# A fill on GpSimd after each gather, and one four-bank PSUM tile for the counts of a step, in a recommendation model's kernel

## The chip, the cores and the metric

The kernel runs on one core of a Trainium2 chip. The metric is the device time of that core in microseconds (us), the median of the runs shown.

## The reference

For each of 16384 rows the model averages 32 word vectors of 300 numbers, averages 20 vectors of 64 numbers from each of three tables, takes one vector of 64 from each of four small tables, and feeds the 748 numbers through three layers. Beside this it sums one scalar per lookup (the "wide" part).

```python
tok = word_emb[token_idx].mean(axis=1)          # 50000 x 300, 32 per row
e1 = emb_mh1[mh1_idx].mean(axis=1)              # 1000 x 64, 20 per row
e2 = emb_mh2[mh2_idx].mean(axis=1)              # 5000 x 64
e3 = emb_mh3[mh3_idx].mean(axis=1)              # 10000 x 64
o1, o2, o3, o4 = emb_oh1[oh1_idx], ...          # 100, 50, 20, 1000 x 64
emb = concatenate([tok, e1, e2, e3, o1, o2, o3, o4], axis=1)
wide = wide_mh1[mh1_idx].sum(...) + ... + wide_oh4[oh4_idx][:, 0]
h = relu(emb @ W1 + b1)                         # 748 x 1024
h = relu(h @ W2 + b2)                           # 1024 x 512
h = relu(h @ W3 + b3)                           # 512 x 256
return sigmoid(h @ Wd + bd + wide)
```

## The kernel before

The batch is cut into 128 tiles of 128 rows. The main loop (L444) runs over tiles, and each tile has 11 steps (`STEPS`), of which each handles six rows from each half of the tile (`ONEHOT` = 6; the last step has four). Three streams are woven together by hand: the framework keeps the order in which the instructions are written, and `Paced` (L411) spreads a stream's work evenly over the steps.

The word vectors come by gather. `tokens` (L205) issues, for each of the 32 words of a tile, one indirect DMA from GpSimd's queue (L212) that fetches 128 rows of 300 numbers. Two gathers share a buffer `tok_rows`, of which there are six. With a lag of three pairs, `add_up` (L197) adds the two halves and then adds them to `g`, both on VectorE (L202, L203). Sixteen pairs are spread over 11 steps.

The small tables stay on the chip, split into 138 slices of 128 rows (`n_h` = 138) and held as three bf16 terms. For each row of the batch, the kernel counts how often each table entry is looked up. `one_hots` (L272) builds, on VectorE, two one-hot arrays for six rows of both halves: `row1` (entry within a slice) and `slice1` (which slice), one step ahead, in two buffers. `counts` (L288) multiplies them: for each row one matmul of 64 x 128 by 64 x 138 into the PSUM tile `pc`, 12 in a full step (L298). A `pc` tile has two banks, one for each half of the tile, and takes three rows of each; so a step of six rows fills two `pc` tiles, and ScalarE evicts each with one ACTIVATE of 828 columns (L305) to `cnt`, fp8. There are two `pc` tiles in the pool `ps_c`. The last step's four rows go as three and one.

One tile later, `small_sums` (L313) multiplies the counts with the tables' terms: 138 matmuls of 195 columns per tile (L323) into `pg`, followed by a VectorE sum of the three terms (L330).

The layers run on blocks of four tiles. `transposed` (L358) turns the block's `g` with TensorE (L366) and scales it on VectorE (L367). `mlp` (L388) and `layer` (L368) then run 88 matmuls of 512 columns in fp32 per block (L376; two records each in the trace), with ReLU evictions on ScalarE (L385), spread over the steps of the next block, and a last layer at L399 to L403. The first block's layers start after the fourth tile's counts are summed; the last blocks are cut smaller (two tiles, one, one).

[...] In a step the written order is: one-hots of the next step, this step's count matmuls and evictions, gathers with older sums, small-table sums, layer matmuls.

Of the kernel before, what the change touches and what calls it, by code (L numbers as in the profile page):

```python
# [8 lines left out]
F32 = mybir.dt.float32  # L9
# [4 lines left out]
AF = mybir.ActivationFunctionType  # L14
# [3 lines left out]
P = 128  # L18
# [3 lines left out]
D1, D2, D3 = 1024, 512, 256  # L22
TOK_GROUP = 2
TOK_LAG = 3
BLOCK = 512
HALF = P // 2
N_SMALL = 3 * N_MH + 4
# [17 lines left out]
def kernel(  # L45
# [21 lines left out]
    nc = tc.nc  # L67
    B = out.shape[0]
    NSUB = BLOCK // P
    M1, M2, M3 = D1 // P, D2 // P, D3 // P  # L70
# [3 lines left out]
    slices, n_h = {}, 0  # L74
    for f in SMALL:
        n = -(-tables[f].shape[0] // P)
        slices[f] = (n_h, n_h + n)
        n_h += n
    PER_BANK = 512 // n_h

    tokp = ctx.enter_context(tc.tile_pool(name="tok", bufs=2 * TOK_LAG))
    const = ctx.enter_context(tc.tile_pool(name="const", bufs=1))
# [6 lines left out]
    wp = ctx.enter_context(tc.tile_pool(name="wide", bufs=2 * NSUB))  # L89
    xp = ctx.enter_context(tc.tile_pool(name="x", bufs=1))  # L90
    ps_h = ctx.enter_context(tc.tile_pool(name="ps_h", bufs=2, space=bass.MemoryType.PSUM))
    ps_c = ctx.enter_context(tc.tile_pool(name="ps_c", bufs=2, space=bass.MemoryType.PSUM))
    ps_g = ctx.enter_context(tc.tile_pool(name="ps_g", bufs=2, space=bass.MemoryType.PSUM))


# [16 lines left out]
    scale = const.tile([P, NK], F32, name="scale")  # L112
# [14 lines left out]
    at = 0  # L127
# [65 lines left out]
            nc.sync.dma_start(out=sb, in_=dram)  # L193

    under_way = []

    def add_up(rows, g, first):  # L197
        a, b, n = rows[:, 0:TOK_D], rows[:, TOK_D : 2 * TOK_D], TOK_D
        if first:
            nc.vector.tensor_add(g[:, 0:n], a, b)  # L200
        else:
            nc.vector.tensor_add(a, a, b)  # L202
            nc.vector.tensor_add(g[:, 0:n], g[:, 0:n], a)  # L203

    def tokens(g, it):  # L205


        for q in range(N_TOK // TOK_GROUP):
            rows = tokp.tile([P, TOK_GROUP * TOK_D], F32, name="tok_rows")
            for t in range(TOK_GROUP):  # L210
                j = q * TOK_GROUP + t
                nc.gpsimd.indirect_dma_start(  # L212
                    out=rows[:, t * TOK_D : (t + 1) * TOK_D],
                    out_offset=None,
                    in_=word,
                    in_offset=bass.IndirectOffsetOnAxis(ap=it[:, j : j + 1], axis=0),
                )
            under_way.append((rows, g, q))
            if len(under_way) > TOK_LAG:
                rows, to, old_q = under_way.pop(0)  # L220
                add_up(rows, to, old_q == 0)
            yield 1
# [5 lines left out]
    def load_indices(blk):  # L228


        b0 = blk * BLOCK
        it = idxp.tile([P, NSUB, N_TOK], I32, name="it")
        nc.sync.dma_start(
            out=it, in_=idx[b0 : b0 + BLOCK, 0:N_TOK].rearrange("(s p) c -> p s c", p=P)
        )
# [36 lines left out]
    def one_hots(sc, s, i):  # L272

        b = i * ONEHOT
        rows = min(ONEHOT, HALF - b)
        row1 = ohp.tile([P, ONEHOT, P], BF16, name="row1")
        slice1 = ohp.tile([P, ONEHOT, n_h], BF16, name="slice1")
        for w, (one, n) in enumerate(((row1, P), (slice1, n_h))):
            shape = [P, rows, n // 2, 2]
            nc.vector.tensor_tensor(  # L280
                one[:, 0:rows, :].rearrange("p i (n d) -> p i n d", d=2),
                iota[:, 0:n].rearrange("p (n d) -> p n d", d=2).unsqueeze(1).to_broadcast(shape),
                sc[:, s // 2, w, s % 2, b : b + rows, :].unsqueeze(2).to_broadcast(shape),
                ALU.is_equal,
            )
        return row1, slice1

    def counts(cnt, hot, i):  # L288

        b = i * ONEHOT  # L290
        rows = min(ONEHOT, HALF - b)
        for k0 in range(0, rows, PER_BANK):
            n = min(PER_BANK, rows - k0)
            pc = ps_c.tile([P, 2, 512], F32, name="pc")
            for k in range(n):
                for f in range(2):
                    half = slice(f * HALF, (f + 1) * HALF)
                    nc.tensor.matmul(  # L298
                        pc[:, f, k * n_h : (k + 1) * n_h],
                        hot[0][half, k0 + k, :],  # L300
                        hot[1][half, k0 + k, :],
                        start=True,
                        stop=True,
                    )
            nc.scalar.activation(  # L305
                cnt[:, :, b + k0 : b + k0 + n, :].rearrange("l f k h -> l f (k h)"),
                pc[:, :, 0 : n * n_h],
                AF.Copy,
                scale=0.5,
                saturate=True,  # L310
            )

    def small_sums(g, cnt):  # L313

# [43 lines left out]
    def transposed(gs):  # L358

        n = len(gs) * P  # L360
        x = xp.tile([P, NK, BLOCK], F32, name="x", tag="even")
        for k in range(NK):
            kk = chunk_k[k]
            pt = ps_h.tile([P, BLOCK], F32, name="pt", tag="ph")
            for s, g in enumerate(gs):
# [6 lines left out]
    def layer(dst, weights, bias, src, kks, n_out, n):  # L372
        for m in range(n_out):
            ph = ps_h.tile([P, BLOCK], F32, name="ph", tag="ph")
            for k, kk in enumerate(kks):
# [66 lines left out]
    hot = one_hots(sc, 0, 0)  # L442
    gs, wides, layers, before, b0 = [], [], None, None, 0
    for t in range(tiles + 1):  # L444
# [4 lines left out]
        if t < tiles:  # L449
            if s == 0 and t:  # L450
                it, sc = next_it, next_sc
            g = gp.tile([P, G_COLS], F32, name="g")
            cnt = cp.tile([P, 2, HALF, n_h], FP8, name="cnt", tag="counts")
            toks = Paced(tokens(g, it[:, s, :].bitcast(U32)), N_TOK // TOK_GROUP, STEPS)
        else:
            last_tokens()
        for i in range(STEPS):
            if t < tiles:
                hot_now = hot
                if s == 1 and i == 0 and t + NSUB < tiles:  # L460
                    next_it, ix = load_indices(t // NSUB + 1)
                if s == 2 and i == 0 and t + NSUB < tiles + 1:
                    next_sc = lookup_keys(ix)
                if i < STEPS - 1:
                    hot = one_hots(sc, s, i + 1)
                elif t + 1 < tiles:
                    hot = one_hots(next_sc if s == NSUB - 1 else sc, (s + 1) % NSUB, 0)
                counts(cnt, hot_now, i)
                if t == 0 and i % 3:
                    next(tables_on_chip, None)  # L470
                if t == 0 and i == STEPS - 1:
                    load_weights()
                toks.go()
            if sums:
                sums.go()
            if layers:
                layers.go()
# [55 lines left out]
```

## Time and profile before

| | |
|---|---|
| plain runs | 5515.67, 5517.34, 5519.1 us; median 5517.34 |
| profiled execution, its own time | 7368.99 us |
| span of the profile | 7367.2 us, mean granted TensorE clock 0.891 |
| busy, TensorE matmul / VectorE / ScalarE / GpSimd | 5894.3 / 3606.2 / 2632.3 / 4079.8 us |
| share of the span | 80% / 49% / 36% / 55% |
| DMA | 652.52 MB, of it 629.41 MB by the gathers' queue, 31.1% of 16 engines' span |

The profiled execution took 1852 us more than a plain one, so its totals and shares don't hold for plain runs as they stand. A row of the page's groups names line, engine and operation, what is written and read, the shape and the count, then busy time and mean of one (ns), then the idle time just before and what ended most of it. PE is TensorE, DVE VectorE, ACT ScalarE, POOL GpSimd; a trailing q is an engine's sequencer or queue. "issue" is time in which an engine waited for nothing that the profile shows.

### The profile page before, as it was taken

To read this page: it belongs to the slowest core of one execution; us is meant where nothing else is said; L and a number is where in the kernel's file an instruction comes from. 1 tells how busy PE (TensorE), PEld (TensorE's weight loads), DVE (VectorE), ACT (ScalarE), POOL (GpSimd) and SP (SyncE) were. 2 spreads that over 40 slices of the span, in tenths; PEclk is the share of its full clock that TensorE was granted. 3 is DMA by queue.
4 is the path that set the end of the run, shared out by engine and by line. 5 is a ranking of instruction groups with operands and counts; after the bars stand their busy time and mean duration, and the time that the engine had idled before them with its cause. 6 is when DMAs were issued, how large, how long until landed. Compare 5 with 4: busy or idle time off the path is not lost.

```text
span 7367.2 us, 103052 instructions
## 1 busy us (share of the span) xinstructions
PE 5894.3 (80%) x41320; PEld 3527.7 (48%) x41320; DVE 3606.2 (49%) x8013; ACT 2632.3 (36%) x3408; POOL 4079.8 (55%) x4103
## 2 busy tenths in 40 slices
PE   3688788878778888878888888888888788888789
PEld 2444444444444444444444444444444444444457
DVE  5544454445454454445444544454445454545443
ACT  4333333333333333333333333333333333333333
POOL 5555555555555555555555555555555555555552
PEclk8789888899898998889888889888988898888999
DMA  5333333333333333333333333333333333333331
GB/s 138 89 90 91 87 87 88 87 90 85 89 86 90 90 88 90 86 89 86 93 86 88 87 90 91 87 87 89 89 89 89 86 90 90 86 91 87 90 87 45
DMA packets 245345, 652.52 MB, mean 89 GB/s; under 512 B 108978, under 2 KB 111989, under 8 KB 244864
## 3 DMA queue, kind: packets, MB, share of 16 engines
q0 software_dynamic: 196608, 629.41, 31.1%
q1 hardware_dynamic: 48255, 16.53, 1.0%
q8 instruction: 323, 5.29, 0.3%
q14 instruction: 159, 1.29, 0.1%
HBM read 645.59 MB, written 0.07 MB: 88 GB/s over the span
## 4 chain that ended last, share of the span: by engine, by line
PE 52%; another core or an unknown queue 26%; ACT 13%; issue 5%; DVE 3%; POOL 0%; DMA 0%; DVEq 0%; SPq 0%; ACTq 0%; POOLq 0%
PE ph L376 24%; PE pg L323 17%; ACT cnt L305 12%; PE pc L298 9%; ACT h L385 1%; PE pt L366 1%; DVE x L367 1%; PE po L399 1%; DVE g L330 0%; PE po L403 0%; DVE slice L280 0%; DVE tok_rows L202 0%; DVE g L203 0%; ACT terms L166 0%
## 5 line engine op out<-in xcount | busy, mean ns | idle before, releaser
L212 POOL DMA_INDIRECT tok_rows<-in_word_emb_dram,it x4096 | 4078.9, 996 | 3207.7 <-DVE g L203 2195.9
L305 ACT ACTIVATE cnt<-pc 128x828 fp8e3<-128x828 f32 (+1 forms) x2816 | 2224.6, 842 | 3325.2 <-PE pc L298 1393.4
L323 PE MATMUL pg<-terms,cnt 128*128 128x195 bf16 x17664 | 2135.3, 271 | 272.0 <-issue 257.2
L280 DVE TENSOR_TENSOR row<-iota,sc 128x768 bf16<-128x768 bf16 (+1 forms) x1408 | 764.7, 543 | 2673.5 <-remote 1282.8
L323 PEld LDWEIGHTS <-cnt 128*128 128x128 fp8e3 x17664 | 1759.2, 147 | 502.7 <-issue 363.6
L298 PE MATMUL pc<-slice,row 64*128 64x138 bf16 x16384 | 880.2, 232 | 1047.6 <-ACT cnt L305 883.0
L376 PE MATMUL ph<-x,w_sb 128*128 128x512 f32 (+5 forms) x3264 | 1625.2, 626 | 43.7 <-issue 41.5
L298 PEld LDWEIGHTS <-row 64*128 64x128 bf16 x16384 | 570.1, 97 | 2182.3 <-issue 1611.2
L376 PE MATMUL ph<-h,w_sb 128*128 128x512 f32 (+2 forms) x2720 | 1404.9, 645 | 26.5 <-issue 24.7
L203 DVE TENSOR_TENSOR g<-g,tok_rows 128x300 f32<-128x300 f32 x1920 | 904.6, 471 | 65.6
L202 DVE TENSOR_TENSOR tok_rows<-tok_rows 128x300 f32<-128x300 f32 x1920 | 890.4, 464 | 0.0
L376 PEld LDWEIGHTS ph<-x,w_sb 128*128 128x128 f32 (+1 forms) x3264 | 610.5, 211 | 516.7 <-issue 505.3
L280 DVE TENSOR_TENSOR slice<-iota,sc 128x828 bf16<-128x828 bf16 (+1 forms) x1408 | 803.8, 571 | 0.0
L385 ACT ACTIVATE h<-ph,b_sb 128x512 f32<-128x512 f32 (+2 forms) x476 | 315.4, 663 | 1225.4 <-remote 739.8
L376 PEld LDWEIGHTS ph<-h,w_sb 128*128 128x128 f32 x2720 | 524.4, 217 | 422.9 <-issue 420.5
L330 DVE TENSOR_REDUCE g<-pg 128x130 f32<-128x390 f32 (+1 forms) x512 | 249.8, 509 | 827.9 <-remote 392.0
L367 DVE TENSOR_SCALAR x<-pt,scale 128x512 f32<-128x512 f32 (+4 forms) x204 | 140.9, 717 | 111.1 <-PE pt L366 104.4
L366 PE MATMUL pt<-ident,g 128*128 128x128 f32 (+1 forms) x768 | 124.8, 292 | 51.8 <-DVE x L367 51.4
L366 PEld LDWEIGHTS pt<-ident,g 128*128 128x128 f32 (+1 forms) x768 | 84.5, 143 | 91.7 <-DVE x L367 83.8
L305 ACT ACT_TABLE_LOAD x32 | 41.1, 1283 | 145.8 <-PE pc L298 145.0
L399 PE MATMUL po<-h,wd_sb 128*1 128x512 f32 (+2 forms) x136 | 62.0, 573 | 0.6 <-issue 0.3
L200 DVE TENSOR_TENSOR g<-tok_rows 128x300 f32<-128x300 f32 x128 | 59.2, 463 | 0.0
(32 smaller groups left out, 346.4 us busy)
## 6 DMA issues: line engine op xcount, KB each, us to landing
tok_rows<-in_word_emb_dram,it POOLq DMA_INDIRECT x4096
ix<-in_idx_dram SPq DMA_DIRECT2D x128, 32.0 KB
w_sb<-in_W_dram SPq DMA_DIRECT2D x6, 512.0 KB
it<-in_idx_dram SPq DMA_DIRECT2D x32, 64.0 KB
w_sb<-in_W_dram SPq DMA_DIRECT2D x1, 2048.0 KB
raw<-in_mh_dram SPq DMA_DIRECT2D x1, 975.0 KB
out_dram<-h SPq DMA_DIRECT2D x31, 2.0 KB
raw<-in_mh_dram SPq DMA_DIRECT2D x1, 292.5 KB
```

The lines of the kernel that those rows point to most:

```text
L202: nc.vector.tensor_add(a, a, b)
L203: nc.vector.tensor_add(g[:, 0:n], g[:, 0:n], a)
L212: nc.gpsimd.indirect_dma_start(out=rows[:, t * TOK_D : (t + 1) * TOK_D], out_offset=None, in_=word, in_offset=bass.IndirectOffsetOnAxis(ap ...
L280: nc.vector.tensor_tensor(one[:, 0:rows, :].rearrange("p i (n d) -> p i n d", d=2), iota[:, 0:n].rearrange("p (n d) -> p n d", d=2).unsque ...
L298: nc.tensor.matmul(pc[:, f, k * n_h : (k + 1) * n_h], hot[0][half, k0 + k, :], hot[1][half, k0 + k, :], start=True, stop=True,)
L305: nc.scalar.activation(cnt[:, :, b + k0 : b + k0 + n, :].rearrange("l f k h -> l f (k h)"), pc[:, :, 0 : n * n_h], AF.Copy, scale=0.5, sat ...
L323: nc.tensor.matmul(pg[:, j, :], by_slice[:, :, h], terms[:, h, :], start=(h == h0), stop=(h == h1 - 1))
L330: nc.vector.tensor_reduce(g[:, at : at + n * ROW].rearrange("p (f d) -> p f d", f=n), pg[:, 0:n, :].rearrange("p f (c d) -> p f d c", c=3) ...
L366: nc.tensor.transpose(pt[:kk, s * P : (s + 1) * P], chunk(g, k), ident)
L367: nc.vector.tensor_scalar(x[:kk, k, 0:n], pt[:kk, 0:n], scale[:kk, k : k + 1], None, ALU.mult)
L376: nc.tensor.matmul(ph[:, 0:n], weights[:kk, k, m * P : (m + 1) * P], src[:kk, k, 0:n], start=(k == 0), stop=(k == len(kks) - 1),)
L385: nc.scalar.activation(dst[:, m, 0:n], ph[:, 0:n], AF.Relu, bias=bias[:, m : m + 1])
```

## The change

Two edits are made together. After each gather, GpSimd fills an SBUF tile `pause` of 128 partitions by 128 fp32 columns with zeros; nothing reads the tile. And the counts of a step go into one `pc` tile of four banks: two for each half of the tile, each bank holding half of the step's rows (three, or two in the last step). One ACTIVATE of 1656 columns (1104 in the last step) evicts all of it. The pool `ps_c` now has one buffer in place of two, so it holds four banks as before.

```diff
+PAUSE = 128
-    PER_BANK = 512 // n_h
-    ps_c = ctx.enter_context(tc.tile_pool(name="ps_c", bufs=2, space=bass.MemoryType.PSUM))
+    ps_c = ctx.enter_context(tc.tile_pool(name="ps_c", bufs=1, space=bass.MemoryType.PSUM))
+    pause = const.tile([P, PAUSE], F32, name="pause")
 def tokens(g, it):
...
                 nc.gpsimd.indirect_dma_start(
...
                 )
+                nc.gpsimd.memset(pause, 0.0)
 def counts(cnt, hot, i):
...
-        for k0 in range(0, rows, PER_BANK):
-            n = min(PER_BANK, rows - k0)
-            pc = ps_c.tile([P, 2, 512], F32, name="pc")
-            for k in range(n):
-                for f in range(2):
-                    half = slice(f * HALF, (f + 1) * HALF)
-                    nc.tensor.matmul(
-                        pc[:, f, k * n_h : (k + 1) * n_h],
-                        hot[0][half, k0 + k, :],
-                        hot[1][half, k0 + k, :],
-                        start=True,
-                        stop=True,
-                    )
-            nc.scalar.activation(
-                cnt[:, :, b + k0 : b + k0 + n, :].rearrange("l f k h -> l f (k h)"),
-                pc[:, :, 0 : n * n_h],
-                AF.Copy,
-                scale=0.5,
-                saturate=True,
-            )
+        n = rows // 2
+        pc = ps_c.tile([P, 2, 2, 512], F32, name="pc")
+        for k in range(rows):
+            for f in range(2):
+                half = slice(f * HALF, (f + 1) * HALF)
+                at = k % n * n_h
+                nc.tensor.matmul(
+                    pc[:, f, k // n, at : at + n_h],
+                    hot[0][half, k, :],
+                    hot[1][half, k, :],
+                    start=True,
+                    stop=True,
+                )
+        nc.scalar.activation(
+            cnt[:, :, b : b + rows, :].rearrange("l f (g k) h -> l f g (k h)", g=2),
+            pc[:, :, :, 0 : n * n_h],
+            AF.Copy,
+            scale=0.5,
+            saturate=True,
+        )
```

## The prediction

> **What bounds the kernel now.** I read the page first, then the chain of waits, then a timeline of all engines in mid-kernel, then GpSimd alone, because the profiled execution took 7369 us (span 7367.2) and the three plain runs 5517. A rate may be taken from this profile only where the profile itself does not stretch it.
>
> ```profile
> PE 52%; another core or an unknown queue 26%; ACT 13%; issue 5%; DVE 3%; POOL 0%; DMA 0%; DVEq 0%; SPq 0%; ACTq 0%; POOLq 0%
> L212 POOL DMA_INDIRECT tok_rows<-in_word_emb_dram,it x4096 | 4078.9, 996 | 3207.7 <-DVE g L203 2195.9 <-issue 876.6 <-DVE g L200 64.8
> L305 ACT ACTIVATE cnt<-pc 128x828 fp8e3<-128x828 f32 (+1 forms) x2816 | 2224.6, 842 | 3325.2 <-PE pc L298 1393.4
> ```
>
> 26% of the span, 1915 us, hangs on a releaser that the profile does not know. One such piece, from the chain in order of time (start, length, what):
>
> ```profile
> 3742.11 1.61 ACT cnt L305 x2
> 3743.72 3.76 another core or an unknown queue
> 3747.49 0.02 issue
> ```
>
> 7367 less 1915 is 5452, within 1.2% of the plain median, so I take these stalls to be what profiling adds (inferred) and work with stretches that lie between them. Here is one (start, length, engine, line, out<-in, count, idle before):
>
> ```profile
> 3720.79 0.54 PE L298 MATMUL pc<-slice,row 64*128 64x138 bf16 x12
> 3721.19 1.61 ACT L305 ACTIVATE cnt<-pc 128x828 fp8e3<-128x828 f32 x2 [1.58 <-PE pc L298]
> 3721.26 1.34 PE L323 MATMUL pg<-terms,cnt 128*128 128x195 bf16 x13
> 3722.45 1.91 PE L376 MATMUL ph<-x,w_sb 128*128 128x512 f32 x4
> ...
> 3724.28 0.54 PE L298 MATMUL pc<-slice,row 64*128 64x138 bf16 x12
> 3724.65 0.95 POOL L212 DMA_INDIRECT tok_rows<-in_word_emb_dram,it  x1 [0.30 <-DVE g L203]
> ...
> 3725.90 0.95 POOL L212 DMA_INDIRECT tok_rows<-in_word_emb_dram,it  x1 [0.30 <-issue]
> ...
> 3727.16 0.95 POOL L212 DMA_INDIRECT tok_rows<-in_word_emb_dram,it  x1 [0.30 <-issue]
> ```
>
> Two rates are to be seen. TensorE repeats a step every 3.49 us (3720.79 to 3724.28) without a hole. GpSimd starts a gather every 1.25 us, also without a hole: the 0.30 us before each belongs to it, since it is there whatever the gather waited for. A step needs 32/11 = 2.91 gathers, so 3.64 us at 1.25. GpSimd is the slower of the two.
>
> Over the kernel: in the 3544 gathers that follow the one before by no more than 0.35 us, start-to-start averages 1.308 us (0.302 gap, 1.003 gather). 4096 x 1.308 = 5357. The last gather starts 80 us before the end and about 20 us are lost in the first tile (one 18.3 us wait for the first sum). 5357 + 80 + 20 = 5457, 60 below the plain 5517; 1.322 us per gather would close it. TensorE: 1408 steps x 3.49 = 4914, plus per block of four tiles some 8 us of transposes and last layer (3708.5 to 3716.3), x 32 = 250, plus about 120 idle in the first five tiles: 5290. So GpSimd is **full to about 1%**, and TensorE has some 200 us to spare. The busy share of the page (POOL 55%) hides this: it leaves out the gap and is diluted by the stalls. The same dilution makes GpSimd look idle behind VectorE:
>
> ```profile
> POOL tok_rows L212 <- DVE g L203: 2195.9, 1064, 9.8
> PE pc L298 <- ACT cnt L305: 883.0, 621, 8.1
> ```
>
> These rows (total us, times, longest) consist mostly of waits of 2 us and more, which is the length of the stalls; between them the waits are absent.
>
> **What the Trainium skill says.** GPSIMD Engine Reference, 3.1 (Elementwise), gives 1.03 cycles per element for a simple body, and 2.1 (Instruction dispatch) tens of cycles of software per instruction. Estimate for 128 columns at the 1.2 GHz that it states: 110 ns plus 25 to 70. The trace has a 128-column fill of 205 ns and one-column fills of 99 to 119, so 96 ns for 127 columns: it agrees. Perfetto Trace Analysis, section DMA Instruction — SWDGE (GPSIMD), says that DSPs 0 and 1 write the descriptors and that the gather's row ends when the last has done so; its section on GPSIMD instructions says to time by start-to-start spacing, which I do. ScalarE: Activation LUTs, What ACT_TABLE_LOAD costs, prices an ACTIVATE with immediates at 186 ns + 0.833 per element: 876 for 828, the trace has 863.
>
> **Part 1, 4096 fills.** One `memset` of 128x128 f32 after each gather, on the engine that has nothing to spare. It adds no DMA and no reader, and nobody waits for `pause`. A fill over an older fill may wait for that one, which ended a gather earlier: nothing. What queues behind it is the next gather, hence its landing, the VectorE sums, and the one-hots that stand behind the sums in VectorE's queue, hence TensorE. The rows that price it are at the kernel's start (GpSimd alone):
>
> ```profile
> 0.28 0.10 POOL L518 MEMSET const-float32-1.0<- 128x1 f32 x1
> 0.30 0.11 POOL L518 MEMSET const-bfloat16-1.0<- 128x1 bf16 x1
> 0.33 0.12 POOL L518 MEMSET const-uint8-127<- 128x1 uint8 x1
> 0.74 0.20 POOL masks.py:197 MEMSET ident<- 128x128 f32 x1 [0.29 <-POOLq L518]
> 0.99 0.23 POOL L121 IOTA iota_i<- 128x138 int32 x1
> ```
>
> One-column fills start 20 to 30 ns apart though each lasts 100, so the tail of a fill overlaps the next instruction. A 128-column one then occupies about 0.03 + 0.096 = 0.125 us; its whole row is 0.205; the IOTA after it starts 0.25 later. Below these lies zero, if the fill fits in the 0.30 us gap; above, 0.205 + 0.302 = 0.507, if the gap is paid twice; a gain is excluded only for this part, since it adds work to the full engine. I choose **0.165**, between occupancy and whole row. 4096 x 0.165 = 676 us, all on the path. The period becomes about 1.32 + 0.165 = 1.49, or 4.32 us per step, against TensorE's 3.49.
>
> A small credit: gathers take 0.945 us where VectorE rests and up to 1.15 beside its two-input sums. VectorE's work is unchanged and spread over a longer time, so the mean lengthening (about 0.06 us) shrinks by some 10%: 4096 x 0.006 = 25, of which I take 15.
>
> **Part 2, the counts of a step.** Removed: 2816 ACTIVATEs (2688 of 863 ns, 128 of 408). Added: 1280 of 1656 columns and 128 of 1104. At 186 + 0.833 per column these are 1.57 and 1.11 us. A full step goes from the 1.61 seen for the pair to 1.57: 0.04 less on ScalarE, which has slack (36% busy). TensorE's 12 matmuls stay. New is the wait: with one buffer of four banks in place of two of two, the first count matmul of a step waits for the previous step's eviction, and the layer and sum matmuls queue behind it. The eviction now starts after 12 matmuls instead of 6, some 0.6 us into the step in place of 0.40, and ends near 2.2; the next count matmul stands 3.49 after the first now, 4.3 after the change. Slack 1.3 us, and still about 1.0 when a 0.69 us `h` eviction just ahead delays it. Worth 0. In tiles 1 to 4, without layers, the gathers set 3.8 us and more per step, so the cover holds there. In tile 0, ScalarE also converts tables at 1.47 us each; a delay of up to 1 us in 11 steps is at most 11 us. If the fills were free and the cover thinner, 0.2 us per step would be 280 us, of which the 200 spare in TensorE takes most. I count 0, with -5 to +11.
>
> **Sum.** On the plain median: 5517 + 676 - 15 + 0 = 6178 us, 12% slower. In the profiled execution the same fills may partly vanish into waits that are there anyway: 7369 plus 0 to 676, perhaps 7700.
>
> **Rivals.**
> *The fill is free (not slower).* In the 0.30 us between gathers, if this gap is the sequencer preparing the next gather while the cores rest, a fill of 0.125 to 0.205 fits in. It decides as long as the fill is shorter than the gap. For it: the gap is constant. Against it: gathers released late by VectorE also start about 0.27 us after the release (3738.58 to 3738.86), where the fill at 0.74 starts together with the first work of ScalarE, so the gap looks like gather code on the cores; and GpSimd's sequencer already runs its 17 ns wait for a later gather at 14.0, just after a gather began at 13.88. Time: 5517, with -10 to +11. A partial fit (0.05 us left) gives 5720.
> *The gap is paid twice.* Alternating two kinds of instruction could cost a second start. For it: no row shows a gather after a fill. Against it: fill to IOTA is 0.25 in all. Time: 5517 + 4096 x 0.507 = 7594; half of the gap, 0.35, gives 6950.
> *TensorE is the bound, GpSimd isn't.* Then GpSimd's own sum at the lowest price rules: 4096 x (1.308 + 0.125) + 100 = 5970, still slower.
> *The single buffer stalls TensorE.* Priced above; behind gathers at 4.3 us per step it would need a wait over 0.6 us in every step to show.
>
> **How the numbers follow.** A measurement of this kernel tells about 0.2% (11 us) from no change. Serial fill at 0.105 to 0.25 us (5930 to 6540): 0.72. Free fill: 0.11, of which 0.08 within 0.2% and 0.03 faster. Partial fit: 0.05. Dearer than 0.25: 0.12. Slower in all: 0.89. The range 5890 to 6750 leaves out the free and most of the partly hidden case below, and part of the dear case above: about 0.2.
>
> **What would show it.** Right: start-to-start of gathers rises from 1.25 to 1.38-1.50 between stalls, with 4096 fills in between; TensorE shows waits before `pc` or one-hots that trace back to VectorE sums and gathers; one ACTIVATE of about 1.57 us per step, ending over 1 us before the next `pc`. Wrong: spacing still near 1.25 (free fill) or over 1.6 (gap twice); TensorE waiting for L305's eviction in ordinary steps between stalls (part 2 is not free).

## The result, and the profile after

The changed kernel takes 5879 us (median of four runs, 5876 to 5884) against 5517 for the kernel before: ratio 1.0657, 95% interval 1.0638 to 1.0675, slower by 362 us. Forecast were 6178 us, 661 more than before, and a range of 5890 to 6750: the direction and the engine were right, the amount was about 1.8 times too large.

The chips fall into two kinds: one runs the kernel before in 5516 to 5525 us, the other in some 7180 to 7250 (a single execution took 9409), and the profile of before shown above (7369 us) is like the second kind while the plain runs above and the profile after are like the first.

The page of the changed kernel: the chain by engine, then the groups (line, engine, operation, out<-in, count, busy us, mean ns, idle before).

```profile
POOL 44%; DMA 28%; DVE 11%; issue 8%; PE 8%; POOLq 0%; ACT 0%; DVEq 0%; SPq 0%; ACTq 0%
...
L214 POOL DMA_INDIRECT tok_rows<-in_word_emb_dram,it x4096 | 4129.0, 1008 | 773.9 <-issue 556.8
L308 ACT ACTIVATE cnt<-pc 128x1656 fp8e3<-128x1656 f32 (+1 forms) x1408 | 2122.4, 1507 | 2466.6 <-PE pc L301 2280.2
...
L220 POOL MEMSET pause<- 128x128 f32 x4096 | 905.9, 221 | 2.2
```

The chain runs through GpSimd, the landing of its gathers and VectorE's sums. The unknown releaser is gone from it. 4129.0 + 905.9 + 773.9 + 2.2 = 5811 of the span's 5882 us are accounted for by gathers, fills and the idle time before them. Of the 4095 stretches between the end of a gather and the start of the next, 4041 have the same length, 0.384 us; the other 54 add up to 118 us; most stand in the first 80 us and the last 125 us of the gathers, the rest are one of 1.0 to 1.7 us every 150 us or so. So GpSimd is full from the first gather to the last, but for some 100 us. GpSimd alone (start, length, ..., idle before):

```profile
3005.03 0.22 POOL L220 MEMSET pause<- 128x128 f32 x1
3005.42 1.01 POOL L214 DMA_INDIRECT tok_rows<-in_word_emb_dram,it  x1 [0.16 <-issue]
3006.42 0.22 POOL L220 MEMSET pause<- 128x128 f32 x1
3006.81 0.95 POOL L214 DMA_INDIRECT tok_rows<-in_word_emb_dram,it  x1 [0.17 <-issue]
3007.75 0.23 POOL L220 MEMSET pause<- 128x128 f32 x1
3008.14 0.95 POOL L214 DMA_INDIRECT tok_rows<-in_word_emb_dram,it  x1 [0.16 <-DVE g L204]
```

Two undisturbed gathers now start 1.33 us apart (6.81 to 8.14), where they started 1.25 apart before. The fill follows the gather at once; after it the next gather waits 0.17 us, where it used to wait 0.30 after a gather. So a fill whose row, its own length in the profile, is 0.22 us makes the period longer by only 0.08. All engines in the same stretch:

```profile
3002.85 0.55 PE L301 MATMUL pc<-slice,row 64*128 64x138 bf16 x12
...
3003.44 1.55 ACT L308 ACTIVATE cnt<-pc 128x1656 fp8e3<-128x1656 f32 x1 [1.95 <-PE pc L301]
...
3006.44 0.54 PE L301 MATMUL pc<-slice,row 64*128 64x138 bf16 x12
```

The eviction of 1656 columns runs from 0.59 to 2.14 us into the step and the next `pc` matmul follows 1.4 us later. And who waits for whom (total us, times, longest):

```profile
DVE tok_rows L203 <- DMA tok_rows<-in_word_emb_dram,it: 1708.2, 1294, 4.1
...
POOL tok_rows L214 <- DVE g L204: 185.0, 831, 9.7
...
PE pc L301 <- DVE slice L283: 281.4, 225, 4.3
...
PE pc L301 <- ACT cnt L308: 60.3, 16, 8.9
```

The waits have changed sides. In the profile of before, GpSimd seemed to wait for VectorE; now VectorE waits 1708 us for gathers to land, and TensorE waits for one-hots behind those sums. TensorE waited for an eviction 16 times, all of them within the first 160 us.

### The profile page after: what moved, and what is told of

The parts are those of the page before. It is cut to its first block, busy times and chain, and to the rows that moved or that the text cites. A ratio compares the mean times of both kernels' runs of the same rounds, so it can differ in the third digit from the quotient of the medians.

```text
span 5882.0 us, 105740 instructions
## 1 busy us (share of the span) xinstructions
PE 5272.8 (90%) x41320; PEld 3219.4 (55%) x41320; DVE 3669.7 (62%) x8013; ACT 2552.0 (43%) x2000; POOL 5026.1 (85%) x8199
## 3 DMA queue, kind: packets, MB, share of 16 engines
q0 software_dynamic: 196608, 629.41, 38.8%
## 4 chain that ended last, share of the span: by engine, by line
POOL 44%; DMA 28%; DVE 11%; issue 8%; PE 8%; POOLq 0%; ACT 0%; DVEq 0%; SPq 0%; ACTq 0%
POOL tok_rows L214 36%; DMA tok_rows<-in_word_emb_dram,it 28%; POOL pause L220 8%; DVE tok_rows L203 5%; DVE g L204 5%; PE ph L379 3%; PE pg L326 2%; PE po L402 1%; DVE x L370 1%; PE pt L369 1%; PE pc L301 1%; PE po L406 0%; POOLq L214 0%; DMA raw<-in_mh_dram 0%; DVE g L333 0%
## 5 line engine op out<-in xcount | busy, mean ns | idle before, releaser
L214 POOL DMA_INDIRECT tok_rows<-in_word_emb_dram,it x4096 | 4129.0, 1008 | 773.9 <-issue 556.8
L308 ACT ACTIVATE cnt<-pc 128x1656 fp8e3<-128x1656 f32 (+1 forms) x1408 | 2122.4, 1507 | 2466.6 <-PE pc L301 2280.2
L326 PE MATMUL pg<-terms,cnt 128*128 128x195 bf16 x17664 | 1881.7, 257 | 160.1 <-DVE g L333 159.8
L326 PEld LDWEIGHTS <-cnt 128*128 128x128 fp8e3 x17664 | 1623.7, 145 | 317.3 <-issue 163.5
L379 PE MATMUL ph<-x,w_sb 128*128 128x512 f32 (+5 forms) x3264 | 1488.2, 584 | 0.0
L301 PEld LDWEIGHTS <-row 64*128 64x128 bf16 x16384 | 509.8, 96 | 1380.6 <-DVE slice L283 605.6
L379 PE MATMUL ph<-h,w_sb 128*128 128x512 f32 (+2 forms) x2720 | 1258.4, 589 | 0.0
L301 PE MATMUL pc<-slice,row 64*128 64x138 bf16 x16384 | 769.9, 226 | 342.5 <-DVE slice L283 281.4
L220 POOL MEMSET pause<- 128x128 f32 x4096 | 905.9, 221 | 2.2
L379 PEld LDWEIGHTS ph<-h,w_sb 128*128 128x128 f32 x2720 | 470.9, 196 | 317.5 <-issue 315.6
```

Of the source, the lines that this page charges most:

```text
L214: nc.gpsimd.indirect_dma_start(out=rows[:, t * TOK_D : (t + 1) * TOK_D], out_offset=None, in_=word, in_offset=bass.IndirectOffsetOnAxis(ap ...
L220: nc.gpsimd.memset(pause, 0.0)
L301: nc.tensor.matmul(pc[:, f, k // n, at : at + n_h], hot[0][half, k, :], hot[1][half, k, :], start=True, stop=True,)
L308: nc.scalar.activation(cnt[:, :, b : b + rows, :].rearrange("l f (g k) h -> l f g (k h)", g=2), pc[:, :, :, 0 : n * n_h], AF.Copy, scale=0 ...
L326: nc.tensor.matmul(pg[:, j, :], by_slice[:, :, h], terms[:, h, :], start=(h == h0), stop=(h == h1 - 1))
L379: nc.tensor.matmul(ph[:, 0:n], weights[:kk, k, m * P : (m + 1) * P], src[:kk, k, 0:n], start=(k == 0), stop=(k == len(kks) - 1),)
```

## The experiments

E1 to E10 and E13 to E18 ran on chips where the kernel before takes 7204 to 7232 us, E11 and E12 on one where it takes 5522. Each ratio is against the kernel before on the same chip. "Gap" is from the end of a gather to the start of the next; its usual length is the median of those of at most 0.6 us. What all longer ones together have beyond it is called the excess. A chip "with stalls" is one of the 7200 us kind. On record these are three chips, two of them met twice, and E11's and E12's is a fourth, met once; which chips ran the main comparison is not on record. Whether the chip itself makes the difference, or something else that stays the same while one is in use, was not tested.

**E1 and E15, the fill alone.**

```diff
                 nc.gpsimd.indirect_dma_start(...)
+                nc.gpsimd.memset(pause, 0.0)
```

> The kernel before with the 128-column fill after each gather and nothing else (two PSUM tiles of two banks stay). If the whole cost is the fill on a full GpSimd: 5879 us as with both edits, within 12 us, and gathers 1.39 us apart when back to back. If the single four-bank PSUM tile has a share: lower by that share. If the PSUM edit hid part of the fill's cost: higher, up to 6178.

> The 128-column fill alone, as in e1. Where before takes about 5520: 5879, the whole change, if the fill is all of it. Where before takes about 7220: 6984, as in e1.

Measured: 6984 us against 7228, ratio 0.967 (0.965 to 0.970); again 6959 against 7204, 0.967 (0.964 to 0.970). On these chips the fill makes the kernel faster. No branch of E1's expectation foresaw that, since all took 5517 as the base; E15's was written after E1.

**E2, E14 and E17, the PSUM edit alone.** The function `counts` and `bufs=1` of the change, with no `pause`.

> The kernel before with the four-bank PSUM tile in one buffer and its one eviction, no fills. If it is worth nothing, as predicted: 5517 us, -5 to +11, gathers 1.31 us apart. If the eviction stalls TensorE enough to reach the path: above 5530. Open question beside it: the profile of before has some 1900 us of stalls on a releaser it does not know, the profile after almost none; if the number of ScalarE evictions brings them, this profiled execution is near its plain time; if the missing fills bring them, it is near 7370 us.

> The four-bank PSUM tile alone, as in e2. Where before takes about 5520: 5515 to 5535 if it is worth nothing; the rest of 362 us if it has a share. Where before takes about 7220: 7220, as in e2.

> The four-bank PSUM tile alone once more, for a chip on which the kernel before takes about 5520. There: 5515 to 5535 if the edit is worth nothing, so that the fill is the whole 362 us. Where before takes about 7200: 7186 to 7231, as in e2 and e14.

Measured: 1.0002 (0.9991 to 1.0013), 0.9964 (0.9950 to 0.9978) and 0.9980 (0.9967 to 0.9993). So between nothing and 0.4% faster here, not measurably slower, and the stalls stay. The chain of E2:

```profile
PE 49%; another core or an unknown queue 29%; ACT 14%; DVE 4%; issue 3%; ACTq 0%; DMA 0%; DVEq 0%; SPq 0%; POOL 0%; POOLq 0%
```

It is much the chain of before (52%, 26%, 13%): half the number of ScalarE evictions doesn't remove the stalls. None of the three runs met a chip without stalls; E12 stands in for it below.

**E3 and E16, a fill of one column; E7, of 32; E4, of 256.**

Against E1:

```diff
-PAUSE = 128
+PAUSE = 1      # E3, E16; 32 in E7, 256 in E4
```

> The kernel before with a fill of one column after each gather. Occupancy theory: the fill holds GpSimd for about 0.03 us, and a gather after a fill starts 0.265 us after it instead of 0.302 after a gather, so nothing is left: 5490 to 5530 us. If each extra instruction has a fixed price (a second start): the 88 ns per gather that the change cost minus 96 ns of columns is below zero, so this theory needs columns to be free, and would give about 5879 us here too.

> The one-column fill after each gather, as in e3. Where before takes about 5520: hidden-share theory 5520, within 15 us; a price per instruction of 0.03 us would give 5640. Where before takes about 7220: 7250, as in e3.

> The kernel before with a fill of 32 columns after each gather. From the gaps of e2, e3, e1 and e4 (0.306 without a fill, 0.305, 0.386 and 0.491 us after fills of 1, 128 and 256 columns): 0.82 ns per column over a hidden share of some 30 columns. Hidden-share theory: gap 0.305 to 0.310, time within 0.4% of before. If every column costs alike from the first: gap 0.325 and 80 us more where GpSimd bounds.

> The kernel before with a fill of 256 columns after each gather. Occupancy theory: 128 more columns at 0.76 to 0.83 ns are 97 to 106 ns, times 4096 = 400 to 435 us over the 128-column fill: 6280 to 6315 us. If the cost were a fixed price per instruction: 5879 us. If GpSimd were not the bound, less than proportional.

Measured: one column 7255 us, ratio 1.0037 (1.0027 to 1.0047), and 7246, 1.0051 (1.0034 to 1.0067); 32 columns 7243, 1.0012 (1.0001 to 1.0024); 256 columns 6346, 0.878 (0.875 to 0.880). The total times mix the fill's price with the stalls, but the gaps do not. E3 with one column, and E4 with 256, GpSimd alone:

```profile
4009.66 0.96 POOL L214 DMA_INDIRECT tok_rows<-in_word_emb_dram,it  x1 [0.19 <-issue]
4010.61 0.12 POOL L220 MEMSET pause<- 128x1 f32 x1
4010.92 0.95 POOL L214 DMA_INDIRECT tok_rows<-in_word_emb_dram,it  x1 [0.19 <-issue]
```

```profile
3103.00 0.33 POOL L220 MEMSET pause<- 128x256 f32 x1
3103.49 0.95 POOL L214 DMA_INDIRECT tok_rows<-in_word_emb_dram,it  x1 [0.17 <-issue]
```

With a one-column fill the next gather starts 0.30 us after the gather before it has ended (10.62 to 10.92), as it does without a fill. The medians together, in us:

| columns of the fill | 0 (E2) | 1 (E3) | 32 (E7) | 128 (after) | 192 (E12) | 256 (E4) |
|---|---|---|---|---|---|---|
| row of the fill | | 0.113 | 0.139 | 0.219 | 0.273 | 0.326 |
| from its end to the next gather | | 0.191 | 0.166 | 0.165 | 0.164 | 0.165 |
| gap | 0.305 | 0.305 | 0.305 | 0.384 | 0.438 | 0.491 |

In these runs the next gather starts at the later of two times: 0.305 us after the gather before it has ended, or 0.165 us after the fill has ended. **A fill costs only what its row has beyond 0.305 - 0.165 = 0.140 us.** From 128 to 256 columns each costs (0.491 - 0.384) / 128 = 0.84 ns. That line meets 0.305 at 128 - 0.079 / 0.00084 = 34 columns, and 32 columns were measured to be free. No price per instruction shows in the gap. The 0.4 to 0.5% of E3 and E16 lies elsewhere: E16's profile beside that of the kernel before on the same chip (E13) has 14 us more of gathers and 10 us more of excess. 256 columns took longer than expected (6346 against 6280 to 6315) mostly because gathers became longer, 1.016 us on average against 1.008 with 128.

**E5, both edits, where the kernel before has stalls.**

> Both edits together, beside the kernel before on the same chip, because the runs of e1 to e4 had the kernel before at 7228 us and not at 5517. Theory A (the two edits add up, and the PSUM edit is worth nothing): where the kernel before takes about 7228, this takes what the fill alone took, 6984; where before takes 5517, it takes 5879. Theory B (fewer TensorE-to-ScalarE hand-overs also shorten the stalls): where before takes about 7228, clearly under 6984, down to 5880. On a chip without stalls A and B agree.

Measured: 6978 us, 0.9676 (0.9659 to 0.9692). Theory A holds: the same as the fill alone. The kernel of the change is thus 6.6% slower on one kind of chip and 3.2% faster on the other.

**E6, one gather in eight left out; E11, every second.**

The main lines:

```diff
+                if t == 1 and q % 4 == 3:      # E11: if t == 1
+                    continue
```

> The kernel before with one gather in eight left out (the second of every fourth pair; the first half is added to itself in its place, so VectorE's work stays), so the word sums are not the reference's. On a chip where before takes 5517: GpSimd's sum falls by 512 x 1.31 = 670 us to about 4790 plus 100, so TensorE's floor shows: 5200 to 5300 us. If GpSimd is not the bound there: 5517. On a chip where before takes about 7228: if the stalls need gathers back to back, they shorten by more than the 670 us; if the stalls are TensorE's own, the time stays within 200 us of 7228.

> The kernel before with every second gather left out (the first of each pair is added to itself in its place, so VectorE's work stays; the word sums are not the reference's). GpSimd is then busy about half the time and cannot be the bound. If gathers close together bring the stalls: TensorE's own floor shows, 5200 to 5350 us, whatever the kernel before takes on that chip. If the stalls belong to the chip and not to the gathers: about 7200 where before takes 7230.

E6: 6502 us, 0.902 (0.900 to 0.903), 704 less for 512 gathers, 1.37 us each: slightly more than the 670 of GpSimd's own sum, so hardly a shortening of stalls beyond it. E11 ran on a chip without stalls: 5252 us, 0.951 (0.950 to 0.953). Its page:

```profile
PE 5100.2 (97%) x41320; PEld 3139.0 (60%) x41320; DVE 3606.2 (69%) x8013; ACT 2632.0 (50%) x3408; POOL 2002.3 (38%) x2055
...
PE 92%; DVE 6%; DMA 1%; issue 0%; ACT 0%; SPq 0%; DVEq 0%; ACTq 0%
```

With the gathers thinned, TensorE is busy 97% and holds 92% of the chain. This is its floor: 5252. The kernel before stands 270 us above it. Not all of that need be the gathers' own: the granted clock was 0.997 in E11 and 0.985 in the kernel before beside it. In the three profiles without stalls TensorE's busy time grows as the clock falls (5100 us at 0.997, 5273 at 0.965 after, 5302 at 0.960 in E12, each product between 5085 and 5090), so an estimate for 0.985 is 5165, or 65 us more than E11; some 205 of the 270 are left to the gathers. E11 cannot say whether thinner gathers would end the stalls, since its chip had none.

**E12, a fill of 192 columns**, on the same chip as E11.

> The kernel before with a fill of 192 columns after each gather: gap by the line through 128 and 256 columns 0.44 us. Where GpSimd alone bounds: 5517 + 4096 x 0.14 = 6090 us. Where before takes about 7230: if the stalls end once the gap passes some point between 0.386 and 0.491, either about 6100 (past it) or about 6900 (short of it); if they fade evenly, about 6660.

Measured: 6006 us, 1.088 (1.086 to 1.090), against 6090 expected from the gap alone. This run has the old PSUM tiles and no stalls, so it is the partner of the changed kernel, though with a longer fill: the fill of 128 columns alone, and the PSUM edit alone, never ran on a chip without stalls. In both, the last gather starts 80.4 us before the end, so each whole time is that of its gathers:

| | gap | mean gather | 4095 starts apart | last gather to end | span |
|---|---|---|---|---|---|
| after (128 columns, four banks) | 0.384 | 1.008 | 1.416 | 80.4 | 5882.0 |
| E12 (192 columns, two banks) | 0.438 | 0.986 | 1.445 | 80.4 | 6001.0 |

The small rest between gap plus gather and the spacing, 0.02 us, is the same in both: it is the 54 longer gaps that each run has, 118 us in all after and 112 in E12. Waits that the PSUM edit puts before gathers can cost no more than a few us, then. Where TensorE waits for evictions, in the first 160 us, it waits 60.3 us after (the line is shown above) and less in E12:

```profile
PE pc L301 <- ACT cnt L308: 35.5, 11, 10.3
```

The single tile brings 25 us more of waiting there, but the 33rd gather starts at 78.0 us after and at 76.7 in E12: 1.3 us reach the path. By the 65th both stand at the same time (122.67 and 122.74), but E12's longer fills account for up to 32 x 0.054 = 1.7 us of what it lost meanwhile, so the 1.3 us are not shown to be made up for.

Gathers are longer after (1.008 us) than in E12 (0.986), 90 us over the kernel. On chips with stalls the PSUM edit doesn't lengthen them: with the 128-column fill they average 0.993 us with the edit (E5), 0.992 and 0.996 without (E1, E15).

**E8, a fill after every second gather; E9, four gather buffers in place of six; E10, rows of 100 numbers in place of 300.**

The main lines of each:

```diff
+                if t == 0:                                              # E8
+                    nc.gpsimd.memset(pause, 0.0)
-    tokp = ctx.enter_context(tc.tile_pool(name="tok", bufs=2 * TOK_LAG))
+    tokp = ctx.enter_context(tc.tile_pool(name="tok", bufs=TOK_LAG + 1))   # E9
-                    in_=word,
+                    in_=word.rearrange("v (c n) -> (v c) n", n=NARROW),    # E10
```

> The kernel before with the 128-column fill only after the first gather of each pair. If the fill's cost adds up one by one: half of the 362 us of the change where before takes 5517 (5700). Where before takes about 7210: if the stalls end with any pause, 6978 or less; if they shrink in proportion to the pauses, about halfway, 7090.

> The kernel before with four gather buffers in place of six, so that GpSimd can run at most some two gathers ahead. Where before takes 5517: GpSimd loses slack, 5517 to 5900. Where before takes about 7210: if the stalls of the other engines last as long as GpSimd's run of gathers lasts, shorter runs shorten them, and this is faster than 7210; if the stalls have nothing to do with the length of the run, the lost slack shows and it is slower.

> The kernel before with gathers of rows of 100 numbers in place of 300 (the word sums are not the reference's; VectorE adds the same 300 columns by repeating the 100). Same number of gathers and rows, a third of the bytes. If descriptors on GpSimd set the pace: gathers stay 1.25 to 1.31 us apart and a chip with before at 5517 shows 5450 to 5517. Where before takes about 7210: if the volume of the gathers' data brings the stalls, they go and the time falls towards 5500; if the number of gathers and of their semaphore updates brings them, 7100 to 7210.

Measured: E8 7169 us, 0.9925 (0.990 to 0.995), a fifth of the fill's gain and not half. E9 7222, 0.9992 (0.998 to 1.0005): the length of GpSimd's run doesn't matter, nor do two of its buffers. E10 7037, 0.973 (0.970 to 0.975): a third of the gathers' bytes (209.98 MB in place of 629.41) takes a tenth of the stalls away, and gathers stay 1.32 us apart where they follow one another. So rows and not bytes set GpSimd's pace, and bytes are not the stalls' main cause. (The edit also changes what VectorE's sums read and write, and its indices reach only the first third of the table.)

**E13 and E18, the kernel before, for its profile.**

> The kernel before itself, for a profile on whichever chip this is: chips of e1 to e10 ran it at 7206 to 7232 us with stalls, that of e11 and e12 at 5522. Where it takes about 5520: GpSimd back to back for all but some 100 us between the first and the last gather, spacing about 1.32 us (4096 x 1.32 + 100 = 5507), TensorE clock near 0.985, no pieces of the chain on an unknown releaser. Where it takes about 7220: as the profile shown.

> The kernel before for its profile, once more. Where it takes about 5520: GpSimd back to back for all but some 100 us between first and last gather, spacing about 1.32 us, no waits of 2 us and more in mid-kernel. Where it takes about 7200: as the profile shown.

Both met chips with stalls: 7209 us and 7204, equal to their partners (1.001 and 0.999). A profile of the kernel before on a chip without stalls is missing from this study.

## Why the prediction was right, and where it was wrong

**GpSimd is full in the kernel before: right.** Two changes show it, though no profile of the kernel before on a chip without stalls does: with half the gathers the time falls to 5252 (E11), and a fill that lengthens the gap by 0.079 us puts 0.088 us per gather onto the total. The prediction's TensorE sum, 5290, is within 1% of E11; the spare that it put at some 200 us is 270, or some 205 with the clock taken into account. The rival in which TensorE is the bound falls with this, on chips without stalls.

**The price of a fill: wrong, and this is the step that failed.** The sum had 4096 x 0.165; it measured 362 / 4096 = 0.088. The low end of the serial case, 0.105, was too high as well. The prediction added the fill to an unchanged gap: it read the 0.30 us as a start-up that every gather pays after whatever comes before it, "since it is there whatever the gather waited for". The runs show instead that after a fill of 32 columns or more only 0.165 us are left, so that 0.140 us of the fill's row lie inside the gap. Of the row of 0.219 us 0.079 remain, or 4096 x 0.079 = 324 of the 362. (The gap itself was read as 0.302 where the trace has 0.306; the prediction's own gap and gather do not add up to its 1.308.) The price of the columns was estimated well (110 ns for 128; from 1 to 128 columns the row grows by 106), so the error lies in the gap. The choice then moved further the wrong way, from occupancy (0.125) towards the whole row (0.205). What happened is the rival of a partial fit, at 0.079 instead of the 0.05 named; it was given only 0.05 of chance, and the low end of the range, 5890, left it out by 11 us. Undisturbed gathers are 1.33 us apart, below the 1.38 to 1.50 that the prediction named as the sign of being right.

**The credit for fewer collisions with VectorE: wrong in sign, as far as can be worked out.** 15 us were taken off. The kernel before's plain time gives (5517 - 83) / 4095 = 1.327 us per gather; less the gap of 0.307 on average and the same rest of 0.024 it leaves gathers of about 0.996 us (an estimate, since no profile without stalls was taken). After, they average 1.008; in E12, 0.986. So gathers became longer by about 0.01 (some 40 us, the rest of the 362) in the change and shorter in E12. Why is not shown: they overlap VectorE's sums for much the same time in both runs, 0.34 and 0.35 us per gather, so busy shares and overlaps do not foretell it.

**The PSUM edit at nothing, -5 to +11: right, as far as shown.** One eviction of 1549 ns against a pair of 1.61 us, 1.4 us of slack against the 1.3 named, 1.3 us in the first tile. It was never run alone without stalls, so a share in the longer gathers is made unlikely by E1, E5 and E15 but not excluded.

**The stalls of the profile are what profiling adds: not borne out, though the number served.** E11 and E12 were profiled without stalls, and their chip runs the kernel before at 5517 to 5525 us; other chips run it at 7200 each time. So profiling alone does not make the stalls. That 7367 less 1915 came near the plain time was luck: what is left is a chain through TensorE and ScalarE (52% and 13%), with GpSimd at 0%, and it is GpSimd that bounds the plain runs. Leaving the stalls out of the rates was still right for the chips of the forecast, but not for the others: there GpSimd is not the bound, the fill shortens stalls, and the sign turns. The forecast for a profiled execution, 7369 to some 7700, failed for both kinds: the changed kernel took 5884 without stalls and 7009 with them (E5).

On one chip with stalls the account closes. E15's profile against E13's: longer gaps cost 323 us and longer gathers 16, while the excess falls from 1823 to 1224; together 260 us less, and the spans are 7219.9 and 6960.5.

**The rivals.** The free fill is ruled out at 128 columns; for the gap it holds at 1 and 32. The gap paid twice is ruled out: 0.17 us follows a fill. The single buffer does not stall TensorE after the first tiles.

**What stays open** is where the stalls come from on such chips. What the runs show is what they depend on. In the profile of before, TensorE has finished a step's matmuls while ScalarE starts on their results late, and GpSimd's gathers run on at 1.25 us:

```profile
3745.20 0.54 PE L298 MATMUL pc<-slice,row 64*128 64x138 bf16 x12
3745.53 0.95 POOL L212 DMA_INDIRECT tok_rows<-in_word_emb_dram,it  x1 [0.30 <-issue]
3746.78 0.94 POOL L212 DMA_INDIRECT tok_rows<-in_word_emb_dram,it  x1 [0.30 <-issue]
3750.36 0.86 ACT L305 ACTIVATE cnt<-pc 128x828 fp8e3<-128x828 f32 x1 [2.16 <-remote]
```

Of 1188 evictions that found ScalarE idle there, 502 started more than 1 us after the last count matmul had ended, up to 9 us; in the profile after, none of 1211 started more than 0.4 us after it. Longer gaps between gathers shrink the stalls out of proportion: a gap of 0.384 us (E1) leaves some 1245 us of excess against 1847 without a fill (E2), one of 0.491 (E4) leaves 92, about as much as the changed kernel has without stalls (97). Not decisive are the number of evictions (E2), extra GpSimd instructions without a longer gap (E3, E7), the buffers (E9) and, for the most part, bytes (E10). No run isolates the mechanism.

## What to carry to other kernels

Before pricing an instruction inserted on a full engine, take the start-to-start spacing with and without it, not its row: here a 0.22 us row cost 0.08, since 0.14 of it lay in a gap that the next instruction had anyway. Whether such a gap stays when something else comes first can be seen only with something in it; runs with a few lengths of the inserted instruction separate the free part from the price. And when a profiled execution takes a third longer than the plain runs, don't name the cause before the same kernel has been profiled on another chip; here a change that paces one engine won on one kind of chip and lost on the other.

## What the runs showed of the hardware

- A gather of 128 rows by one index per partition had a row of 0.945 us on GpSimd where nothing lengthened it, plus a 0.305 us gap before the next, with rows of 1200 bytes and with rows of 400 bytes alike (mean spacing 1.31 and 1.32, E10).
- With a fill between two gathers the next started at the later of 0.305 us after the gather or 0.165 us after the fill: fills of 1 and 32 columns added nothing to the gap, longer ones 0.84 ns per column beyond about 34.
- The same program took 5516 to 5525 us on some chips and 7180 to 7250 on others; the slower ones show stalls that shrink as the gap between gathers grows (1847 us of excess at 0.305, 1245 at 0.384, 92 at 0.491).
